# Dense attention on one core: products with values in four column groups once a step, and scores, exponentials and maxima in single PSUM banks

## The chip, the core and the metric

The kernel runs on one core of a Trainium2 chip. The metric is the device time of one execution, in microseconds. The program is one launch that holds a whole stack of four blocks, each a half feed-forward part, an attention and a second half feed-forward part.

## The reference

The input x has 4 sequences of 512 rows of 128 features. Every block adds, in turn, half a feed-forward part, an attention and half a feed-forward part, each of the normalized x. Three of these parts hold a *dense* attention with 16 heads of 8 features, and only these are touched here: both feed-forward parts of block 1 (causal, followed by a mixture of 8 experts of which two count) and the attention of block 3 (without a mask).

The lines are block 1's; block 3 has them without the two that make and apply the mask.

```python
scores = jnp.einsum('bhqd,bhkd->bhqk', q, k) * scale
causal = jnp.tril(jnp.ones((S, S), dtype=bool))
scores = jnp.where(causal[None, None], scores, -jnp.inf)
attn = jax.nn.softmax(scores, axis=-1)
ctx = jnp.einsum('bhqk,bhkd->bqhd', attn, v).reshape(B, S, E)
attn_out = ctx @ out_proj_w.T + out_proj_b
```

All is in 32-bit floats. The other parts (gated and pattern feed-forwards, linear, blocked and local attentions) keep their instructions.

## The kernel before

Features lie on the 128 partitions. A head has 8 features; four heads fill a group of 32 partitions, and there are four such groups g. For each of four j, a copy of the keys is kept in which only head j of every group is non-zero (L712 to L723, "marked keys"), so that a product over the 32 partitions of one group gives the scores of one head. A *unit* u is a sequence b and a j, thus four heads, one in each group; there are 16 units. A unit has four *steps* (one block of 128 keys each, kt), and a step has two *halves*, of groups 0, 1 and of groups 2, 3.

`dense_attention` (L748) is a loop over steps n, from -5 on, and over halves. In each half it does in this order, and TensorE keeps the order in which products are written (`mm_in_order`, L163):

- `scores` (L799): two products of a 32x128 block of marked keys with 32x512 queries, for the groups of this half, into the two banks of one PSUM tile `pk_at`, of which there is one (`k=1`).
- `maxima` (L764): for the step five later (LEAD) and for the *other* half's groups, two products of queries with marked keys into the two banks of one tile `pq_at` (`q=2`), from which VectorE takes row maxima into `nm`: one reduction over both banks without a mask (L780), or two masked ones (L785).
- `weights` (L812): ScalarE takes the exponential of the pair in one instruction (L815) into `PT` in SBUF; in the masked case GpSimd then sets the part above the diagonal to 0 (L818).
- `with_values` (L823): for the step before, two products of 128x32 values with `PT`, whose 32-column results go to the column groups g of one bank `po_at` (`o=1`), and add up over the unit's four steps.
- What has been put off (`later`, L870 on, and the chains of `tick`, L265): transposes of the maxima for the queries of the next unit (`queries`, pm_at, L790), the end of a unit (`end`, pt_at, L838), loading of the next sequence (`prepare`), and the experts, normalizations and gates (L968 on).

The masked case treats only what is not masked: score widths go 512, 384, 256, 128 in a unit's four steps. All PSUM is in use: `MIX = dict(k=1, q=2, o=1, m=1)`, where k and q count double banks; m is one bank for everything else. The products of the experts (`products`, L1020) take one of the two `q` tiles, as two halves, and VectorE adds them up in eight instructions (L1033) before the tile is free. Near the start and the end of masked loops, products that nobody reads (`idle_product`, L169) run in a bank of `o` or `q`. The gated feed-forward of block 3 takes a double bank `pag` (L1799) from a pool of its own.

A helper writes every product, so nearly all products carry line L164, and transposes L161.

Of the kernel before, what the change touches and what calls it, by code (L numbers as in the profile page):

```python
# [24 lines left out]
AF = mybir.ActivationFunctionType  # L25
# [78 lines left out]
def tile_macaron(ctx, tc, x_in, const_in, vec_in, w0_in, ws_in, ws3_in, w2f_in, w3_in, out):  # L104
# [15 lines left out]
            yield  # L120

    def bank(tag, name):
        n = 2 if tag in "kqd" else 1
        return psum["pool"].tile([P, n * 512], F32, tag=tag, name=name, bufs=psum["bufs"][tag])

    x = keep.tile([P, NT, D], F32, name="x")
    w0 = keep.tile([P, WA], F32, tag="wa", name="w0")
# [35 lines left out]
    def mm_in_order(dst, lhsT, rhs, start=True, stop=True):  # L163
        tc.keep_in_program_order(nc.tensor.matmul(dst, lhsT=lhsT, rhs=rhs, start=start, stop=stop))  # L164
# [60 lines left out]
    def by_order(i):  # L225
        if ordered["act"]:
            tc.keep_in_program_order(i)
# [477 lines left out]

    LEAD = 5
    VW = HD + 1
    MIX = dict(k=1, q=2, o=1, m=1)  # L710

    def marked_keys(sb, src, bias):  # L712

# [34 lines left out]
    def dense_attention(sb, prepare, finish, wo, masked, tiles=None):  # L748
# [15 lines left out]
        def maxima(step, half):  # L764

            (b, j), qt = units[step // TB], order[step % TB]
            qT, km = seqs[b]["q"], seqs[b]["k"]
            nk = (qt + 1) * P if masked else S
            pq = bank("q", "pq_at")
            for i in range(2):  # L770
                g = half * 2 + i
                mm_in_order(
                    pq[:, i * 512 : i * 512 + nk],
                    qT[32 * g : 32 * g + 32, ts(qt, P)], km[32 * g : 32 * g + 32, j, :nk],
                )
            nm = nms[j % 2]
            if not masked:
                a = nm[:, qt, 0:1]
                to = bass.AP(a.tensor, a.offset + 64 * half + HD * (j ^ 1), [list(a.ap[0]), [32, 2]])
                nc.vector.tensor_reduce(to, pq.rearrange("p (i n) -> p i n", i=2), AX.X, ALU.max)  # L780
                return
            for i in range(2):
                at = 64 * half + 32 * i + HD * (j ^ 1)
                s = sb.tile([P, S], F32, tag="s", name="s")
                nc.vector.tensor_tensor_reduce(  # L785
                    s[:, :nk], pq[:, i * 512 : i * 512 + nk], causal[:, S - nk :], 1.0, -BIG, ALU.add, ALU.max,
                    nm[:, qt, at : at + 1],
                )

        def queries(u):  # L790
            b, j = units[u]
# [7 lines left out]
        def scores(step, half):  # L799

            u, kt = step // TB, step % TB
            b, j = units[u]
            q0 = kt * P if masked else 0
            pk = bank("k", "pk_at").rearrange("p (i n) -> p i n", i=2)
            for i in range(2):
                g = half * 2 + i
                mm_in_order(
                    pk[:, i, q0:], seqs[b]["k"][32 * g : 32 * g + 32, j, ts(kt, P)], qxs[u][32 * g : 32 * g + 32, q0:]
                )
            return pk  # L810

        def weights(step, half, pk):  # L812
            q0 = step % TB * P if masked else 0
            PT = sb.tile([P, 2, S], F32, tag="PT", name="PT", bufs=4)
            by_order(nc.scalar.activation(PT[:, :, q0:], pk[:, :, q0:], AF.Exp, scale=SC8))  # L815
            if masked:
                d = PT[:, :, q0 : q0 + P]
                nc.gpsimd.affine_select(  # L818
                    d, d, pattern=[[0, 2], [1, P]], base=0, channel_multiplier=-1, compare_op=ALU.is_ge, fill=0.0
                )  # L820
            PTs[step, half] = PT

        def with_values(step, half):  # L823
            u, kt = step // TB, step % TB
            b, j = units[u]
            q0 = kt * P if masked else 0
            if kt == 0 and half == 0:
                pos[u] = bank("o", "po_at")
            PT = PTs.pop((step, half))
            for i in range(2):  # L830
                g = half * 2 + i
                at = (4 * g + j) * VW
                mm_in_order(
                    pos[u][32 * g : 32 * g + 32, q0:], seqs[b]["vh"][:, kt, at : at + 32], PT[:, i, q0:],
                    kt == 0, kt == TB - 1,
                )

# [47 lines left out]

        for n in range(-LEAD, n_steps + 5):
            for half in range(2):
                pk = scores(n, half) if 0 <= n < n_steps else None
                if n + LEAD < n_steps:
                    maxima(n + LEAD, 1 - half)  # L890
                if masked and n < 0:
                    idle_product("o", S // 2)
                elif masked and routed and n_steps - LEAD <= n < n_steps:
                    idle_product("q", S // 2)
                if pk is not None:
                    weights(n, half, pk)
                if 1 <= n <= n_steps:
                    with_values(n - 1, half)
                    if half and n % TB == 0:
                        u = n // TB - 1  # L900
                        oTs[u] = sb.tile([P, S], F32, tag="oT", name="oT")
                        by_order(nc.scalar.copy(oTs[u], pos.pop(u)))
                fs = later.pop((n, half), ())
                tick(bool(fs))
                for f in fs:
                    f()
# [61 lines left out]
    def l1_experts(sb, b):  # L968
# [49 lines left out]
            nc.vector.tensor_add(yb, yb, pb.rearrange("p (t d) -> p t d", d=D))  # L1018

        def products(t):  # L1020
            if "e" in psum["bufs"]:
                pe = [bank("e", "pe1") for _ in range(2)]
            else:
                p = bank("q" if "q" in psum["bufs"] else "d", "pe1")
                pe = [p[:, 0:512], p[:, 512:1024]]
            for half in range(2):
                mm_in_order(pe[half], yT[:, b, ts(t, P)], ew[:, ts(half, 512)])
            st["pe", t] = pe
# [544 lines left out]
    def l3_ffn(w3, tag, first, rb):  # L1573
        with pool(tag) as sb, banks(tag + "ps", d=3, m=2):
# [5 lines left out]
            def W(l, name):  # L1580
                return W3(w3, f"{name}{l}")
# [4 lines left out]
            def act(*args, **kw):  # L1586
                tc.keep_in_program_order(nc.scalar.activation(*args, **kw))  # L1587
# [2 lines left out]
                tc.keep_in_program_order(nc.scalar.copy(dst, src))  # L1590

            def pair(name):
                return bank("d" if "d" in psum["bufs"] else "q", name)

            def light(u):

# [81 lines left out]
            def weights(step):  # L1678

                u, t = step // TB, step % TB  # L1680
                qT, kT = s_state[step].pop("qT"), u_state[u]["kT"]
                ps = pair("ps3")
                for fc in range(4):
                    for w in range(2):
                        for r in range(2):
                            at = r * 512 + fc * P
                            k0 = t * P + w * 64
                            mm_in_order(
                                ps[64 * w : 64 * w + 64, at : at + P],
                                qT[64 * r : 64 * r + 64, fc, ts(w, 64)], kT[64 * r : 64 * r + 64, fc, k0 : k0 + P],  # L1690
                            )
# [101 lines left out]
            def hidden(u, c, at=whole):  # L1793
                l, b = units[u]
                a, n = HCH[c]
                h2, w1, m = u_state[u]["h2"][:, at], W(l, "w1"), at.stop - at.start
                if c == 0 and at.start == 0:
                    u_state[u]["hh"] = rb.tile([P, 3, S], F32, tag="hh", name="hh")
                p = pair("pag")  # L1799
                mm_in_order(p[:n, 0:m], w1[:, HID + a : HID + a + n], h2)  # L1800
                mm_in_order(p[:n, 512 : 512 + m], w1[:, a : a + n], h2)
                ge = tmp("ge")
                act(ge[:n, :m], p[:n, 0:m], AF.Gelu, bias=W(l, "b1g")[:n, c : c + 1])
                nc.vector.scalar_tensor_tensor(
                    u_state[u]["hh"][:n, c, at], p[:n, 512 : 512 + m], W(l, "b1a")[:n, c : c + 1], ge[:n, :m], ALU.add, ALU.mult
                )

            def close_unit(u, at=whole):
# [252 lines left out]
```

## Time and profile before

| what | before |
|---|---|
| median of 3 runs | 2833.52 us (2828.96 to 2839.0) |
| the profiled execution, its own time | 2852.98 us |
| its span | 2851.2 us, mean granted clock 0.886 |
| PE, DVE, ACT, POOL busy | 2254.2, 1806.5, 1245.4, 907.3 us |
| first and last pk of the masked attentions | 415.4 to 720.0 us, 901.1 to 1204.6 us |
| first and last pk of the unmasked attention | 2087.4 to 2423.1 us |
| exponentials (L815), all three | 384 instructions, 311.1 us |
| masked maxima (L785), unmasked maxima (L780) | 512 in 248.5 us, 128 in 156.4 us |

PE is TensorE's matrix products, PEld its loads of weights, DVE VectorE, ACT ScalarE, POOL GpSimd. A row of the timeline has the start, the duration, the engine, the line, the operation, what it writes and reads, the shapes, how many instructions are merged into the row, and in brackets how long the engine was idle before it and who ended that. A product in 32-bit floats appears as two MATMUL records. A row of groups has the count, then busy time and mean duration in ns, and after the second bar the idle time before them with those who ended it. PE's durations contain the way through the array, so that rows overlap; the distance between starts tells how fast it takes work.

### The profile page before, as it was taken

How to read it: one execution, taken by the hardware profiler on the slowest of the kernel's cores; microseconds unless marked ns; L12 is line 12 of the kernel's file. 1: busy time of each engine (PE TensorE's matmuls, PEld its weight loads, DVE VectorE, ACT ScalarE, POOL GpSimd, SP SyncE). 2: the span in 40 equal slices, each digit the busy share in tenths (PEclk: the TensorE clock that was granted, in tenths of full speed). 3: DMA queues.
4: the chain of work that ended last, by engine and by line, in shares of the span. 5: the costliest groups of instructions: out<-in, count | busy, mean ns of one | idle time of the engine just before them, and what ended most of it. 6: DMA issues, size and time to landing. Idle time of an engine off the chain costs nothing. (4 is left out here: it accounts for less than half of the span.)

```text
span 2851.2 us, 47230 instructions
## 1 busy us (share of the span) xinstructions
PE 2254.2 (79%) x17676; PEld 1181.4 (41%) x17676; DVE 1806.5 (63%) x4885; ACT 1245.4 (44%) x2683; POOL 907.3 (32%) x1678
## 2 busy tenths in 40 slices
PE   4377468988678898958666768898799999688988
PEld 2155123333334333338456645555322222455555
DVE  4745576675676676463664497777566564777774
ACT  3054314433333433314332256776334444567674
POOL 1023012232122222203322377676200000677661
PEclk8588769998789998968886889999899999999998
DMA  3052010000000000008104511000000000110000
GB/s 137 9 162 68 0 60 1 1 1 1 1 1 1 1 1 5 4 16 290 38 13 174 169 25 24 20 22 16 1 0 1 1 1 1 27 23 20 22 22 12
DMA packets 33917, 99.15 MB, mean 35 GB/s; under 512 B 6200, under 2 KB 12344, under 8 KB 33176
## 3 DMA queue, kind: packets, MB, share of 16 engines
q1 hardware_dynamic: 30760, 88.03, 9.5%
q0 software_dynamic: 2496, 5.12, 0.8%
q8 instruction: 139, 2.28, 0.3%
q10 hardware_dynamic: 432, 2.98, 0.3%
q14 instruction: 90, 0.74, 0.1%
HBM read 66.88 MB, written 14.55 MB: 29 GB/s over the span
## 5 line engine op out<-in xcount | busy, mean ns | idle before, releaser
L815 ACT ACTIVATE PT<-pk_at 128x1024 f32<-128x1024 f32 (+3 forms) x384 | 311.1, 810 | 546.7 <-PE pq_at L164 466.7
L164 PE MATMUL pk_at<-qx,km 32*128 32x512 f32 (+3 forms) x1536 | 366.2, 553 | 58.5 <-ACT PT L815 53.3
L164 PE MATMUL po_at<-PT,vh 128*32 128x512 f32 (+3 forms) x1536 | 329.0, 510 | 4.4 <-POOL PT L818 4.2
L785 DVE CUSTOM_DVE_ANT_0 s<-pq_at,cst 128x384 f32<-128x384 f32 (+3 forms) x512 | 248.5, 485 | 93.9 <-PE pq_at L164 82.4
L1587 ACT ACTIVATE s<-s,nm,rn 128x128 f32<-128x128 f32 x512 | 245.5, 482 | 2.5 <-POOL ir L191 1.9
L818 POOL TENSOR_SCALAR_AFFINE_SELECT PT<-PT 128x256 f32<-128x256 f32 x256 | 106.9, 419 | 417.6 <-ACT PT L815 417.4
L164 PEld LDWEIGHTS pk_at<-qx,km 32*128 32x128 f32 x1536 | 118.8, 188 | 260.7 <-ACT PT L815 198.3
L164 PE MATMUL pq_at<-km,qT 32*128 32x128 f32 (+3 forms) x1024 | 218.4, 503 | 7.6 <-DVE y L1033 3.9
L780 DVE TENSOR_REDUCE nm<-pq_at 128x2 f32<-128x1024 f32 x128 | 156.4, 1225 | 92.1 <-PE pq_at L164 91.9
L1648 POOL TENSOR_TENSOR t<-t,t 128x1024 f32<-128x1024 f32 x64 | 151.7, 2371 | 127.7 <-DVE t L1644 127.4
L161 PE MATMUL pt_y<-ident,y 128*128 128x128 f32 x224 | 52.0, 359 | 136.4 <-DVE y L218 91.5
L164 PE MATMUL p_qk<-w,hT 128*128 128x512 f32 x256 | 137.9, 665 | 16.2 <-DVE hT L1605 9.0
L164 PE MATMUL pq_at<-km,t 32*128 32x512 f32 x512 | 147.5, 653 | 2.0 <-DVE nm L780 2.0
L164 PEld LDWEIGHTS po_at<-PT,vh 128*32 128x32 f32 x1536 | 55.7, 109 | 221.3 <-issue 146.2
L161 PE MATMUL pt<-ident,s 128*128 128x128 f32 x640 | 93.8, 294 | 61.7 <-POOL s L1711 37.4
L1711 POOL TENSOR_TENSOR s<-s,sm 128x1024 f32<-128x1024 f32 x64 | 121.6, 1900 | 49.8 <-DVE sm L1710 41.8
L247 ACT COPY yT<-pt_y 128x512 f32<-128x512 f32 x56 | 32.8, 586 | 235.2 <-PE pt_y L161 235.1
L1587 ACT ACTIVATE sq<-p_qk 128x1024 f32<-128x1024 f32 x64 | 65.7, 1026 | 120.9 <-PE p_qk L164 67.3
L161 PEld LDWEIGHTS pt<-ident,s 128*128 128x128 f32 x640 | 78.8, 151 | 94.1 <-POOL s L1711 48.6
L1641 DVE TENSOR_TENSOR t<-p_qk,w 128x1024 f32<-128x1024 f32 x64 | 78.2, 1222 | 52.9 <-ACT sq L1587 52.6
L1329 DVE SCALAR_TENSOR_TENSOR hT<-pa,w,sg 128x128 f32<-128x128 f32 x184 | 51.8, 345 | 87.4 <-ACT sg L1328 65.5
L161 PEld LDWEIGHTS pt_y<-ident,y 128*128 128x128 f32 x224 | 33.3, 169 | 168.1 <-issue 96.1
(435 smaller groups left out, 5202.5 us busy)
## 6 DMA issues: line engine op xcount, KB each, us to landing
w<-in_w2f_dram SPq DMA_DIRECT2D x46, 836.0 KB, 7.7
vb<-v SPq DMA_DIRECT2D x112, 128.0 KB, 2.2
skew<-qe SPq DMA_DIRECT2D x16, 512.0 KB, 3.0
rel<-skew SPq DMA_DIRECT2D x64, 128.0 KB, 3.7
w<-in_w_dram SPq DMA_DIRECT2D x1, 4147.0 KB, 12.5
w<-in_w_dram SPq DMA_DIRECT2D x1, 3200.0 KB
od<-o SPq DMA_DIRECT2D x46, 64.0 KB, 5.5
yd<-y SPq DMA_DIRECT2D x8, 256.0 KB
```

What stands on the lines that cost most here:

```text
L161: return nc.tensor.transpose(dst, src, ident[: src.shape[0], : src.shape[0]])
L164: tc.keep_in_program_order(nc.tensor.matmul(dst, lhsT=lhsT, rhs=rhs, start=start, stop=stop))
L247: by_order(nc.scalar.copy(yT[:, b, :], pt))
L780: nc.vector.tensor_reduce(to, pq.rearrange("p (i n) -> p i n", i=2), AX.X, ALU.max)
L785: nc.vector.tensor_tensor_reduce(s[:, :nk], pq[:, i * 512 : i * 512 + nk], causal[:, S - nk :], 1.0, -BIG, ALU.add, ALU.max, nm[:, qt, at ...
L815: by_order(nc.scalar.activation(PT[:, :, q0:], pk[:, :, q0:], AF.Exp, scale=SC8))
L818: nc.gpsimd.affine_select(d, d, pattern=[[0, 2], [1, P]], base=0, channel_multiplier=-1, compare_op=ALU.is_ge, fill=0.0)
L1329: nc.vector.scalar_tensor_tensor(hT[s][:, c, :], pa[:, ts(c, P)], b1[:, c : c + 1], sg, ALU.add, ALU.mult)
L1587: tc.keep_in_program_order(nc.scalar.activation(*args, **kw))
L1641: nc.vector.tensor_mul(by_head(t1), by_head(p3), over(tab[:, 0]))
L1648: nc.gpsimd.tensor_add(t1, t1, t2)
L1711: nc.gpsimd.tensor_mul(s, s, bcast(sm, P))
```

## The change

- `k` and `q` become single banks, three of each (`MIX = dict(k=3, q=3, o=1, m=1)`): the same eight banks.
- Every group's scores have a bank of their own, and so have its maxima. Exponentials and unmasked reductions are one instruction per bank (twice as many, half as wide).
- `with_values` is called once a step, after half 1's scores and maxima, with all four groups.
- `two_banks` hands out two banks: halves of a double bank where the pool has `d`, else two single ones. The experts' products and `pag` use it. For `pag` and for the experts outside of the dense attentions that is what they had.

```diff
-        n = 2 if tag in "kqd" else 1
+        n = 2 if tag == "d" else 1
...
+    def two_banks(name):
+
+        if "d" in psum["bufs"]:
+            p = bank("d", name)
+            return p[:, 0:512], p[:, 512:1024]
+        return [bank("e" if "e" in psum["bufs"] else "q", name) for _ in range(2)]
...
-    MIX = dict(k=1, q=2, o=1, m=1)
+    MIX = dict(k=3, q=3, o=1, m=1)
...
-            pq = bank("q", "pq_at")
-            for i in range(2):
+            nm = nms[j % 2]
+            pqs = [bank("q", "pq_at") for _ in range(2)]
+            for i, pq in enumerate(pqs):
                 g = half * 2 + i
...
+                mm_in_order(pq[:, :nk], qT[32 * g : 32 * g + 32, ts(qt, P)], km[32 * g : 32 * g + 32, j, :nk])
...
-                nc.vector.tensor_reduce(to, pq.rearrange("p (i n) -> p i n", i=2), AX.X, ALU.max)
...
+                    nc.vector.tensor_reduce(to, pq, AX.X, ALU.max)
...
-            pk = bank("k", "pk_at").rearrange("p (i n) -> p i n", i=2)
-            for i in range(2):
+            pks = [bank("k", "pk_at") for _ in range(2)]
+            for i, pk in enumerate(pks):
...
-            by_order(nc.scalar.activation(PT[:, :, q0:], pk[:, :, q0:], AF.Exp, scale=SC8))
+            for i, pk in enumerate(pks):
+                by_order(nc.scalar.activation(PT[:, i, q0:], pk[:, q0:], AF.Exp, scale=SC8))
...
-        def with_values(step, half):
+        def with_values(step):
...
-            PT = PTs.pop((step, half))
-            for i in range(2):
-                g = half * 2 + i
+            PT = [PTs.pop((step, half)) for half in range(2)]
+            for g in range(4):
                 at = (4 * g + j) * VW
                 mm_in_order(
-                    pos[u][32 * g : 32 * g + 32, q0:], seqs[b]["vh"][:, kt, at : at + 32], PT[:, i, q0:],
+                    pos[u][32 * g : 32 * g + 32, q0:], seqs[b]["vh"][:, kt, at : at + 32], PT[g // 2][:, g % 2, q0:],
                     kt == 0, kt == TB - 1,
                 )
...
-                if 1 <= n <= n_steps:
-                    with_values(n - 1, half)
-                    if half and n % TB == 0:
+                if half and 1 <= n <= n_steps:
+                    with_values(n - 1)
+                    if n % TB == 0:
...
-            if "e" in psum["bufs"]:
-                pe = [bank("e", "pe1") for _ in range(2)]
-            else:
-                p = bank("q" if "q" in psum["bufs"] else "d", "pe1")
-                pe = [p[:, 0:512], p[:, 512:1024]]
+            pe = two_banks("pe1")
...
-                p = pair("pag")
-                mm_in_order(p[:n, 0:m], w1[:, HID + a : HID + a + n], h2)
-                mm_in_order(p[:n, 512 : 512 + m], w1[:, a : a + n], h2)
+                pg, pa = two_banks("pag")
+                mm_in_order(pg[:n, :m], w1[:, HID + a : HID + a + n], h2)
+                mm_in_order(pa[:n, :m], w1[:, a : a + n], h2)
```

More of the change, by code (lines that the diff above doesn't have):

```diff
@@ L768, in maxima @@
             nk = (qt + 1) * P if masked else S
-            pq = bank("q", "pq_at")
-            for i in range(2):
+            nm = nms[j % 2]
+            pqs = [bank("q", "pq_at") for _ in range(2)]
+            for i, pq in enumerate(pqs):
                 g = half * 2 + i
[L772 to L781, printed above, removed]
-            for i in range(2):
-                at = 64 * half + 32 * i + HD * (j ^ 1)
[L784 to L788, printed above, removed]
+                mm_in_order(pq[:, :nk], qT[32 * g : 32 * g + 32, ts(qt, P)], km[32 * g : 32 * g + 32, j, :nk])
+            for i, pq in enumerate(pqs):
+                at = 64 * half + 32 * i + HD * (j ^ 1)
+                to = nm[:, qt, at : at + 1]
+                if masked:
+                    s = sb.tile([P, S], F32, tag="s", name="s")
+                    nc.vector.tensor_tensor_reduce(s[:, :nk], pq[:, :nk], causal[:, S - nk :], 1.0, -BIG, ALU.add, ALU.max, to)
+                else:
+                    nc.vector.tensor_reduce(to, pq, AX.X, ALU.max)
         def queries(u):
@@ L803, in scores, with weights @@
             q0 = kt * P if masked else 0
-            pk = bank("k", "pk_at").rearrange("p (i n) -> p i n", i=2)
-            for i in range(2):
+            pks = [bank("k", "pk_at") for _ in range(2)]
+            for i, pk in enumerate(pks):
                 g = half * 2 + i
                 mm_in_order(
-                    pk[:, i, q0:], seqs[b]["k"][32 * g : 32 * g + 32, j, ts(kt, P)], qxs[u][32 * g : 32 * g + 32, q0:]
+                    pk[:, q0:], seqs[b]["k"][32 * g : 32 * g + 32, j, ts(kt, P)], qxs[u][32 * g : 32 * g + 32, q0:]
                 )
-            return pk
-        def weights(step, half, pk):
+            return pks
+        def weights(step, half, pks):
             q0 = step % TB * P if masked else 0
             PT = sb.tile([P, 2, S], F32, tag="PT", name="PT", bufs=4)
-            by_order(nc.scalar.activation(PT[:, :, q0:], pk[:, :, q0:], AF.Exp, scale=SC8))
+            for i, pk in enumerate(pks):
+                by_order(nc.scalar.activation(PT[:, i, q0:], pk[:, q0:], AF.Exp, scale=SC8))
             if masked:
@@ L826, in with_values @@
             q0 = kt * P if masked else 0
-            if kt == 0 and half == 0:
+            if kt == 0:
                 pos[u] = bank("o", "po_at")
-            PT = PTs.pop((step, half))
-            for i in range(2):
-                g = half * 2 + i
+            PT = [PTs.pop((step, half)) for half in range(2)]
+            for g in range(4):
                 at = (4 * g + j) * VW
                 mm_in_order(
-                    pos[u][32 * g : 32 * g + 32, q0:], seqs[b]["vh"][:, kt, at : at + 32], PT[:, i, q0:],
+                    pos[u][32 * g : 32 * g + 32, q0:], seqs[b]["vh"][:, kt, at : at + 32], PT[g // 2][:, g % 2, q0:],
                     kt == 0, kt == TB - 1,
@@ L1592, in pair @@
             def pair(name):
-                return bank("d" if "d" in psum["bufs"] else "q", name)
+                return bank("d", name)
             def light(u):
@@ L1798, in hidden @@
                     u_state[u]["hh"] = rb.tile([P, 3, S], F32, tag="hh", name="hh")
-                p = pair("pag")
-                mm_in_order(p[:n, 0:m], w1[:, HID + a : HID + a + n], h2)
-                mm_in_order(p[:n, 512 : 512 + m], w1[:, a : a + n], h2)
+                pg, pa = two_banks("pag")
+                mm_in_order(pg[:n, :m], w1[:, HID + a : HID + a + n], h2)
+                mm_in_order(pa[:n, :m], w1[:, a : a + n], h2)
                 ge = tmp("ge")
-                act(ge[:n, :m], p[:n, 0:m], AF.Gelu, bias=W(l, "b1g")[:n, c : c + 1])
+                act(ge[:n, :m], pg[:n, :m], AF.Gelu, bias=W(l, "b1g")[:n, c : c + 1])
                 nc.vector.scalar_tensor_tensor(
-                    u_state[u]["hh"][:n, c, at], p[:n, 512 : 512 + m], W(l, "b1a")[:n, c : c + 1], ge[:n, :m], ALU.add, ALU.mult
+                    u_state[u]["hh"][:n, c, at], pa[:n, :m], W(l, "b1a")[:n, c : c + 1], ge[:n, :m], ALU.add, ALU.mult
                 )
```

## The prediction

> **What bounds the kernel now.** I read the page first, then the table of windows for the three dense attentions, then the timeline of one half step, then the groups by shape for the prices.
>
> The page says that PE is busy for 79% of 2851.2 us and no other engine for more than 63%; the profiled execution took 2852.98 us, 0.7% over the median 2833.52 of the runs. The change touches three windows only:
>
> ```profile
> 415.00:720.00 305.00, 271.57 (x1812) 103.54 (x1811) 194.61 (x765) 120.08 (x191) 86.48 (x205) 0.94 0.00 1
> 901.00:1205.00 304.00, 273.51 (x1830) 105.32 (x1829) 190.66 (x744) 118.83 (x188) 82.81 (x202) 0.95 0.01 3
> 2087.00:2424.00 337.00, 312.05 (x1710) 84.46 (x1712) 191.56 (x255) 146.12 (x156) 8.89 (x7) 0.99 0.00 1
> ```
>
> The columns are length, then PE, weight loads, DVE, ACT, POOL busy, then the granted clock. PE is busy for 89 to 93% in each: two masked attentions (305 and 304 us) and the unmasked one (337). How a half step of the unmasked one looks (first column the start, second the duration; the weight loads are left out):
>
> ```profile
> 2152.52 0.70 PE L164 MATMUL pk_at<-qx,km 32*128 32x512 f32 x2 [0.19 <-ACT PT L815]
> ...
> 2152.53 0.70 PE L164 MATMUL pq_at<-km,t 32*128 32x512 f32 x2
> ...
> 2153.05 0.59 PE L164 MATMUL pk_at<-qx,km 32*128 32x512 f32 x2
> 2153.06 0.59 PE L164 MATMUL pq_at<-km,t 32*128 32x512 f32 x2
> ...
> 2153.59 1.05 PE L164 MATMUL po_at<-PT,vh 128*32 128x512 f32 x4
> 2153.75 1.23 DVE L780 TENSOR_REDUCE nm<-pq_at 128x2 f32<-128x1024 f32 x1 [1.09 <-PE pq_at L164]
> 2153.75 1.02 ACT L815 ACTIVATE PT<-pk_at 128x1024 f32<-128x1024 f32 x1 [1.29 <-PE pq_at L164]
> ...
> 2154.83 0.70 PE L164 MATMUL pk_at<-qx,km 32*128 32x512 f32 x2 [0.19 <-ACT PT L815]
> ```
>
> Each fp32 product is two passes. Two pk and two pq lie in four row groups and run together: passes begin 0.53 us apart, 1.07 us for all four products. The two po follow in two column groups, also together. Their individual starts are 0.453 us apart per pass, so 0.91 us. PE has then issued 1.98 us of work, and the next pk, which needs the only pk tile, waits until the exponentials of the whole pair have ended. The loop is 1.07 + 0.16 (drain and signal, 2153.59 to 2153.75) + 1.02 + 0.06 = 2.31 us; PE lacks work for 0.33 of it.
>
> From the starts of pk in the timeline, undisturbed steps take 4.62, 4.95, 4.62, 4.95 us in the unmasked attention (19.14 a unit of four; 0.33 twice for the transposes pm and pt) and 4.62, 4.31, 2.92, 2.61 in a masked one (14.46). Sixteen units make 306 and 231 us; the remaining 30 and 74 us are other work of PE in between, a halved clock (about 31 us in each masked window, some 15 us lost), and stalls.
>
> **The change, part by part.**
>
> Products with values. Removed: one of two issues of two column groups per step; added: one issue of four. If four groups run together as two do, a 512-wide step saves 0.91 us. The trace has four groups elsewhere, 128 wide:
>
> ```profile
> 873.33 0.86 PE L164 MATMUL po_1a<-PT,vm 128*32 128x128 f32 x24
> ```
>
> 24 passes in 0.86 us, the last one's drain within it; individual rounds of four start 0.109 us apart (serially 24 x 0.109 = 2.6). [...] I take the row: its rounds show no loss, only its width is other. The moved half-0 products go behind half 1's pk and pq on PE; their PT is a step old, so no wait is added, and oT's copy by ACT follows the fourth product as before.
>
> Banks. A pk bank now comes round every third product, so the fourth product of a step waits for the first one's exponential, where a pair used to wait for the pair. Prices:
>
> ```profile
> L815 ACT ACTIVATE PT<-pk_at 128x1024 f32<-128x1024 f32 x32 | 32.8, 1024 | 65.3 <-PE pq_at L164 52.9 <-PE pk_at L164 10.1 <-POOL PT L818 2.3
> L815 ACT ACTIVATE PT<-pk_at 128x512 f32<-128x512 f32 x32 | 19.1, 596 | 47.5 <-PE pq_at L164 38.8 <-PE pk_at L164 7.2 <-POOL ln_r L198 1.4
> ```
>
> Two of 596 for one of 1024: +0.168 us a pair, 256 x 0.168/2 = 21 us more ACT in the unmasked window (146 of 337 busy, so on no path). DVE's one reduce of 1226 ns becomes two, not shown by the trace; bounds are 0.61 (half) and 0.75 us (the dearest 512-wide DVE row there); I take 0.69, as tensor-tensor rows have at 512 and 1.22 at 1024. [...]
>
> Unmasked step after, from its first pk (t = 0). Half 0 issues until 1.07. Its first exponential runs 1.23 to 1.83, its first reduce 1.23 to 1.92. pk of the third group starts at 1.07 in a fresh bank; the fourth waits for the exponential until 1.88; the first pq behind it needs no more, the second pq waits for the reduce until 1.98. Behind these waits are queued the products with values and all other PE work of the slot; exponentials and reduces of half 1 wait for them too. A later row group may join a running one: at 682 us pq start 0.89 us after pk and pk's second pass begins on time. Half 1 ends at 3.05, four po at 3.96, and the change from column to full mode took 0.08 (po to pt_y, 523.97 to 524.96). So 4.04 us. pt adds 0.6; pm falls into the stall of half 1 and is free (0.6 if DVE is late). Unit: 4 x 4.04 + 0.6 = 16.8 against 19.1: 16 x 2.4 = -38 us.
>
> Masked, by the same chain with rows of their widths (exponentials 0.60, 0.49, 0.38, 0.27; reduces 0.69, 0.54, 0.42, 0.29; pk and pq 1.07, 0.85, 0.64, 0.43; po, a step late, 0.27, 0.91, 0.69, 0.48): 3.4, 4.2 with pt, 2.7, 2.1, together 12.4 against 14.5: 16 x 2.1 = -34 us each. Reduces were separate here before, so DVE has nothing more to do.
>
> What is given back. PE is in order, so lateness of DVE stops it. Before, a pq pair waited for the pair two back (in the unmasked loop some 2.1 us of slack); after, a bank for the third back (0.1 us at worst). Expert products (L1024) took one of two pq tiles and now take two of three banks: the fourth pq after them waits for four of eight sums of 0.35 us. Tracing two cases, I get 0.4 to 1.0 us lost a call, some 12 us a masked window. Other DVE bursts (normalization, choice, km): 60 us of DVE extras a masked window, of which I let a third stall, less what deeper pk banks save when ACT is late: 5 us. Unmasked: 27 us of DVE extras, mostly in bursts, some 4 us net. So -34 + 17 = -17 for each masked window, and -38 + 4 = -34 unmasked. (The other way about, masked: 198 for 16 clean units; 47 of other PE work, counted from the order of instructions at 0.96 to 1.07 a 128x512 product and 0.13 a transpose, of which 20 stand in half 0 and 6 of these hide in the stall; 15 of clock; 28 of stalls, of which some 12 are there now too: 288 against 305.) Bounds: nothing lost (-34, -38) to all DVE extras stalling.
>
> The gated FFN's pag, now through two_banks, gets the same two halves of the same tile and its instructions stay: nothing. The idle products take one bank instead of two, at equal length: nothing. No DMA moves.
>
> Sum: 2 x -17 - 34 = -68 us on the span, carried to the median: 2765 us.
>
> **The rivals.**
>
> 1. DVE lateness decides, slower. All 60 us of DVE extras of a masked window stop PE, and PE's pauses drop the clock: masked 198 + 41 (the 47 less the hidden 6) + 15 + 60 = 314, plus 15 us for twice the cold time: +24 each. Unmasked 268 (16 x 16.8) + 15 (other PE work, 22 less what hides) + 27 = 310: -26. Total +22: 2856. It decides from about 50 us of PE stall per masked window. For it: slack falls to 0.1 us. Against: DVE is busy for only 64%, and PE's waits for DVE are a few us now. Chance 14%.
> 2. The stalls of half 1 fill with the other PE work and bursts hide: masked -40 each, unmasked -45: 2708. Chance 14%.
> 3. [...] Chance 9%.
> 4. It does not do what it says: half 1's waits cost what the po saving brings, 2834. Chance 6%.
> The likeliest, 2765 (2740 to 2800), has 57%.
>
> **How the numbers follow.** A measurement here tells about 0.3% (8.5 us) from no change. Faster by more: likeliest, 2 and 3, 80%; within: 6%; slower: 14%. The range leaves out the far half of rivals 1 and 2: 2708 to 2834.
>
> **What would show it.** After, po should come as eight passes within about 1.05 us, once a step; one pk alone at 1.07 us, its fellow with two pq at 1.9; undisturbed unmasked steps of 4.0 us; windows of about 288, 287 and 303 us. Wrong would be: four po passes of 0.6 us or more apart; PE idle before pq on nm, s or y (DVE) of over 50 us a masked window; a clock under 0.9 there.

## The result, and the profile after

The changed kernel takes 2807.05 us (median of 5 runs, 2792.72 to 2815.06); five runs of the kernel before, the three shown among them, give 2838.25. The ratio is 0.9872 with an interval of 0.9852 to 0.9893: faster by 1.3%, some 31 us in medians, where 68 were forecast. The direction was right, the size about half. Two later measurements of the same pair give 46 and 42 us.

The profiled executions lie further apart than the medians, 2852.98 and 2795.84 us: before's is 14.7 us above the median of its five runs, after's is 11.2 below its own. So 57 us between the two profiles stand for about 31. Some 10 of the 57 lie between the second masked attention and the unmasked one, which the change leaves as it was: that stretch took 882.8 us before, 872.4 here, and 883.2 in both later profiles of the changed kernel. Only what repeats is built on below.

The three windows again, with the same columns (length; PE, weight loads, DVE, ACT, POOL busy; granted clock), each from the first to the last pk of an attention, now of the kernel after:

```profile
416.00:704.00 288.00, 268.86 (x1811) 121.91 (x1814) 200.03 (x767) 129.43 (x319) 86.80 (x205) 0.92 0.00 1
881.00:1184.00 303.00, 285.67 (x1825) 129.66 (x1817) 194.53 (x740) 129.35 (x315) 82.99 (x202) 0.86 0.01 3
2056.00:2364.00 308.00, 290.77 (x1701) 103.73 (x1700) 198.07 (x374) 154.49 (x282) 8.90 (x7) 0.97 0.00 1
```

The first masked attention went from 305 to 288 us, as forecast. The second, which does the same work, stayed at 303 (287 forecast). The unmasked one went from 337 to 308 (303 forecast). The column that moves the wrong way is the clock: 0.94, 0.95, 0.99 before, now 0.92, 0.86, 0.97. It fell most where the gain is missing. And PE is *busier* in the second masked window than before (285.67 against 273.51 us), though the change packs its products with values into less time: instructions at half clock last longer and count as busy (below, eight passes of po in 1.70 us instead of 1.07).

One undisturbed step of the unmasked attention, from the timeline of after (start, duration; weight loads and a few rows left out):

```profile
2107.88 0.70 PE L171 MATMUL pk_at<-qx,km 32*128 32x512 f32 x2
2107.90 0.70 PE L171 MATMUL pq_at<-km,t 32*128 32x512 f32 x2
...
2108.86 1.52 PE L171 MATMUL pk_at<-qx,km 32*128 32x512 f32 x3
2109.04 1.57 ACT L817 ACTIVATE PT<-pk_at 128x512 f32<-128x512 f32 x3 [2.22 <-PE pq_at L171]
2109.13 1.29 DVE L789 TENSOR_REDUCE nm<-pq_at 128x1 f32<-128x512 f32 x2 [0.55 <-PE pq_at L171]
2109.70 0.87 PE L171 MATMUL pq_at<-km,t 32*128 32x512 f32 x2
...
2110.92 1.07 PE L171 MATMUL po_at<-PT,vh 128*32 128x512 f32 x8
2111.92 0.70 PE L171 MATMUL pk_at<-qx,km 32*128 32x512 f32 x2
```

The step has the form that was worked out, and its length: 2107.88 to 2111.92 is 4.04 us. The fourth pk waits for the first exponential, and from 2108.86 one pk runs alone, joined at 2109.70 by pq. Eight passes of po in four column groups take 1.07 us; two groups took 1.05 for four passes. Three exponentials in a row are merged into 1.57 us, so consecutive ones overlap; two reductions take 1.29.

So the undisturbed steps are right, and the loss lies elsewhere. I cut each attention into its 63 steps from one step's first pk to the next one's, and took from the records of granted clock how long each step ran at half clock:

| attention | 63 steps, before to after, us | at half clock, us | steps at full clock in both: number, change | the other steps: change |
|---|---|---|---|---|
| first masked | 301.5 to 283.0 | 34 to 43 | 50: -16.7 us | 13: -1.7 us |
| second masked | 301.1 to 301.3 | 31 to 82 | 41: -16.3 us | 22: +16.5 us |
| unmasked | 332.8 to 306.0 | 5 to 16 | 59: -29.4 us | 4: +2.6 us |

Carried over to all 63 steps, the steps at full clock gain 21, 25 and 31 us (16.7 x 63/50 and so on), together 77. What was had is 45 (the sums of the second column). The steps that ran at half clock in one kernel or the other took the 32 us between.

This is how such a stretch begins: a burst in the unmasked attention, from the timeline of after. Normalization (y), key copies (km) and maxima stand in line on DVE:

```profile
2158.11 2.12 DVE L225 TENSOR_SCALAR y<-x,ln_mv,ln_r 128x128 f32<-128x128 f32 x4
...
2160.15 0.99 DVE L729 TENSOR_SCALAR km<-t,cst 128x512 f32<-128x512 f32 x2
...
2161.07 2.58 DVE L789 TENSOR_REDUCE nm<-pq_at 128x1 f32<-128x512 f32 x4
2161.80 0.69 PE L171 MATMUL pq_at<-km,t 32*128 32x512 f32 x1 [1.96 <-DVE nm L789]
...
2164.04 1.70 PE L171 MATMUL po_at<-PT,vh 128*32 128x512 f32 x8
```

PE waits 1.96 us for a maximum that stands behind the burst; from about 2164 the same eight passes of po take 1.70 us instead of 1.07. The table of windows for three stretches of 4 us around it:

```profile
2156.00:2160.00 4.00, 3.39 (x19) 0.76 (x16) 3.97 (x10) 1.81 (x4) 1.26 (x1) 1.00 0.01 2
2160.00:2164.00 4.00, 2.20 (x10) 1.13 (x10) 3.77 (x8) 3.13 (x6) 0.00 (x0) 1.00 0.00 0
2164.00:2168.00 4.00, 3.23 (x14) 1.34 (x14) 1.69 (x4) 0.41 (x1) 0.00 (x0) 0.54 0.00 0
```

DVE is busy all the time (3.97, 3.77 of 4), PE falls to 2.20 of 4, and 0.54 is the clock of the next 4 us. That the pause brings the low clock is the reading of this place, which shows only the order; what the 25 falls of the clock in the two profiles show follows after the experiments.

How much of the pauses is DVE's lateness, by the table of waits (weight loads in front of pq; us in all, times, longest), first masked attention before:

```profile
PEld pq_at L164 <- DVE y L1033: 5.0, 6, 1.4
PEld pq_at L164 <- DVE nm L785: 4.5, 5, 1.9
```

and after:

```profile
PEld pq_at L171 <- DVE nm L787: 17.7, 21, 3.2
```

9.5 us became 17.7; in the second masked attention 7.5 became 15.3, in the unmasked one 3.7 became 12.8. That is 8 to 9 us more in each, far from the 50 of rival 1, and alike in the two masked attentions. It cannot be what parts 288 from 303. Over all weight loads that wait for DVE, not only those before pq, the three went from 27, 26 and 10 us to 32, 29 and 27: 3 to 4 us more in a masked attention, 17 in the unmasked one.

### The profile page after: what moved, and what is told of

The parts are those of the page before. It is cut to its first block, busy times and chain, and to the rows that moved or that the text cites. A ratio compares the mean times of both kernels' runs of the same rounds, so it can differ in the third digit from the quotient of the medians.

```text
span 2793.4 us, 48072 instructions
## 1 busy us (share of the span) xinstructions
PE 2243.8 (80%) x17676; PEld 1246.5 (45%) x17676; DVE 1820.5 (65%) x5013; ACT 1274.0 (46%) x3067; POOL 909.6 (33%) x1678
## 4 chain that ended last, share of the span: by engine, by line
PE 56%; DVE 23%; POOL 8%; ACT 7%; issue 5%; DMA 2%; POOLq 0%; DVEq 0%; SPq 0%; ACTq 0%
PE pk_at L171 12%; PE po_at L171 5%; PE pq_at L171 4%; PE pa L171 3%; PE pag L171 3%; PE po L171 3%; PE pe L171 2%; DVE t L1638 2%; DVE t L1641 2%; PE p_qk L171 2%; PE pg L171 2%; PE pz L171 2%; PE pv L171 2%; PE pt L168 2%; POOL t L1645 2%
## 5 line engine op out<-in xcount | busy, mean ns | idle before, releaser
L817 ACT ACTIVATE PT<-pk_at 128x512 f32<-128x512 f32 (+3 forms) x768 | 337.3, 489 | 453.1 <-PE pq_at L171 376.1
L171 PE MATMUL pk_at<-qx,km 32*128 32x512 f32 (+3 forms) x1536 | 453.6, 563 | 12.2 <-ACT PT L817 10.0
L171 PE MATMUL pq_at<-km,qT 32*128 32x128 f32 (+3 forms) x1024 | 279.9, 525 | 16.7 <-DVE nm L787 13.7
L171 PEld LDWEIGHTS pk_at<-qx,km 32*128 32x128 f32 x1536 | 170.2, 195 | 226.3 <-ACT PT L817 119.2
L789 DVE TENSOR_REDUCE nm<-pq_at 128x1 f32<-128x512 f32 x256 | 165.2, 684 | 64.3 <-PE pq_at L171 63.5
L171 PE MATMUL po_at<-PT,vh 128*32 128x512 f32 (+3 forms) x1536 | 173.6, 526 | 0.0
L171 PE MATMUL pq_at<-km,t 32*128 32x512 f32 x512 | 166.8, 657 | 6.5 <-DVE nm L789 6.5
L171 PEld LDWEIGHTS pq_at<-km,qT 32*128 32x128 f32 x1024 | 109.4, 197 | 53.5 <-DVE nm L787 35.5
```

The lines of the kernel that those rows point to most:

```text
L789: nc.vector.tensor_reduce(to, pq, AX.X, ALU.max)
L817: by_order(nc.scalar.activation(PT[:, i, q0:], pk[:, q0:], AF.Exp, scale=SC8))
```

## The experiments

My theory after the result: the steps come out as worked, and the missing half goes to the clock, which falls since PE, with less to do, more often pauses. (The last clause did not hold as it stands. By the windows of before and after PE's idle time, the length less its busy time, was 33, 30 and 25 us before and is 19, 17 and 17 after.) Rivals: DVE's lateness itself (the experts' sums above all), and that one of the two parts does not bring what it should.

**The products with values alone.** Before's banks, with the four groups once a step:

```diff
-        def with_values(step, half):
+        def with_values(step):
...
-                if 1 <= n <= n_steps:
-                    with_values(n - 1, half)
-                    if half and n % TB == 0:
+                if half and 1 <= n <= n_steps:
+                    with_values(n - 1)
+                    if n % TB == 0:
```

> The kernel before, with only the products with values changed: once a step, after half 1, in all four column groups; the double banks stay. Theory (the loop from a pk tile through the exponential of the pair and back sets the step, 2.31 us a half): clean unmasked steps stay at 4.62 us, PE only idles longer in half 0, and the time stays within 0.4% of before. Rival (the column groups are the gain): 0.9 us a step less in the unmasked attention, some 30 us in all.

It takes 2846.83 us against 2841.3 (20 and 23 runs): 1.0016 (1.0007 to 1.0026). The timeline of half 1, then the next half 0, without values in between:

```profile
2116.41 0.70 PE L164 MATMUL pk_at<-qx,km 32*128 32x512 f32 x2 [0.17 <-ACT PT L815]
...
2117.64 1.02 ACT L815 ACTIVATE PT<-pk_at 128x1024 f32<-128x1024 f32 x1 [1.29 <-PE pq_at L164]
2118.72 0.70 PE L164 MATMUL pk_at<-qx,km 32*128 32x512 f32 x2 [1.17 <-ACT PT L815]
```

A half is still 2.31 us (2116.41 to 2118.72), since the exponential of the pair closes the loop. The 0.91 us of PE that the column groups save became idle time: PE now waits 1.17 us here instead of 0.19. And the clock is lower, by the table of windows (first masked, unmasked):

```profile
417.00:722.00 305.00, 249.55 (x1806) 102.00 (x1798) 195.16 (x760) 120.19 (x191) 86.66 (x205) 0.88 0.00 1
...
2074.00:2418.00 344.00, 268.95 (x1698) 80.46 (x1700) 191.68 (x252) 146.15 (x155) 8.91 (x7) 0.93 0.00 1
```

PE's busy time fell from 271.57 to 249.55 and from 312.05 to 268.95 us, the clock from 0.94 to 0.88 and from 0.99 to 0.93. Time at half clock in the three attentions' steps went from 34, 31, 5 to 70, 58, 43 us. Steps at full clock in both kernels gained 9.0, 10.8 and 7.9 us (41, 44, 55 steps), the others lost 8.1, 9.8 and 15.1. So what the steps at full clock gained, 28 us, the others lost again, 33 us.

**The banks alone.** After, with the values twice a step again, two groups each:

```diff
-        def with_values(step):
+        def with_values(step, half):
...
-                if half and 1 <= n <= n_steps:
-                    with_values(n - 1)
-                    if n % TB == 0:
+                if 1 <= n <= n_steps:
+                    with_values(n - 1, half)
+                    if half and n % TB == 0:
```

> The changed kernel, with products with values once a half in two column groups again. Theory: PE's 1.98 us a half plus some 0.1 for the change of mode set the pace, since the wait for the first exponential (1.88 us) is over when the two po are issued: clean unmasked steps of 4.15 to 4.2 us against 4.04 of the whole change, so the banks alone bring most of the gain, 20 to 30 us. Rival (column groups are the gain): as before, 2838 us.

2819.44 us against 2841.3: 0.9915 (0.9886 to 0.9944). Its windows:

```profile
418.00:713.00 295.00, 281.57 (x1812) 111.59 (x1810) 199.60 (x767) 128.12 (x318) 86.29 (x205) 0.96 0.00 1
893.00:1188.00 295.00, 285.35 (x1825) 114.99 (x1824) 195.00 (x745) 126.89 (x315) 82.75 (x202) 0.96 0.01 3
2055.00:2388.00 333.00, 320.35 (x1704) 88.10 (x1701) 198.89 (x373) 154.13 (x282) 8.87 (x7) 0.96 0.00 1
```

Undisturbed unmasked steps take 4.11 and 4.69 us, with no wait for the exponential left in the middle of a half. PE is busy 95 to 97% of every window, and both masked attentions are alike, with a clock of 0.96. The same finer buffers, with the same nearness of DVE, but without the saving on PE, hold the clock: 24, 24 and 26 us at half clock, about as much in all as before. Here 0.85% (22 us, as expected most of the gain), in the whole change 1.3 to 1.7% in three measurements, and in the values alone nothing: in the whole time the parts do not add up. In the steps at full clock they come closer: 28 us for the values alone, 22 for the banks alone (4.5, 3.4 and 14.6 in 52, 54 and 59 steps), 62 for both. What hides the values' share when they stand alone is the clock.

**The values between the halves.** After, with the four groups put after half 0:

```diff
-                if half and 1 <= n <= n_steps:
+                if not half and 1 <= n <= n_steps:
```

> The changed kernel, with the four products with values after half 0's scores and maxima instead of after half 1's, to fill PE's wait there. If that wait were a loss that any work fills: unmasked steps of 3.1 to 3.3 us, 45 us less than the changed kernel. Theory (three banks for four products: the second product of the next step waits for this step's third exponential, 1.89 us after half 1 begins): the wait only moves to the next half 0, steps of 3.95 us, the time within 10 us of the changed kernel's 2807.

2793.82 us: 0.9832 (0.9799 to 0.9865). Undisturbed unmasked steps come in a pattern of 3.36, 4.62, 4.04 and 4.72 us, 16.74 us for four, as much as in the changed kernel: the wait only moved, as expected. The windows are 289.8, 284.3 and 320.5. The second masked attention is now the good one (34 us at half clock in its steps, the first 58), and the unmasked one loses (47). A shift of one instruction group moves the spells of half clock from one attention to another, with little change in the total: where they fall is not a property of the second masked attention.

**Work for PE in the pauses.** After, with a product that nobody reads in front of half 1's pk, in a bank that this pk overwrites, so that it fills the wait for the exponential. First in all three attentions:

```diff
+            if half:
+                w = (S - q0) // 2
+                mm_in_order(pks[0][:, q0 : q0 + w], onesm, cst[:, :w])
```

> The changed kernel with one more product a step that nobody reads (full array, half the width of the scores), ahead of half 1's first score product and into its bank, where PE else runs one row group alone or waits. Theory (what is missing of the forecast is the clock, 113 us at half clock in the masked windows against 60 before): less than 70 us of half clock in the masked windows and 15 to 25 us less than the changed kernel. Rival (lateness of VectorE itself is what is missing): the clock is up, the time within 5 us of the changed kernel, clean steps at 4.04 us in both cases.

2782.94 us: 0.9796 (0.9770 to 0.9823), with windows of 284.7, 289.6 and 315.5 us and 58 us at half clock in the masked steps, where the changed kernel has 125. Then only where there is a mask (`if half and masked`):

> The changed kernel with the unread product of the first filled kernel in the two masked attentions only. Theory (the fill pays through the clock, and the unmasked attention was warm without it: there the fill only delays): the unmasked attention is back at about 308 us, the masked ones at 285 to 290, 7 us less than with the fill everywhere: 2776 us. Rival (the fill pays through something other than the clock): no less than with the fill everywhere, 2783 us or more.

2779.67 us against 2837.32: 0.9792 (0.9768 to 0.9817). The unmasked attention is back at 308 us, but the ratio is that of the filling everywhere; the 7 us expected are not shown. On another chip, side by side with the plain change:

> The changed kernel once more, beside the fill on one chip. Theory (clock): mean granted clock about 0.87 against 0.888 before, ratio 0.982 to 0.988.

> The changed kernel with the fill in the masked attentions, on the same chip as the changed kernel. Theory (what is missing is the clock): mean clock 0.88 or more, undisturbed warm steps no shorter, and 0.4 to 0.9% (11 to 25 us) less time than the changed kernel in runs on the same chip. Rival (the gain of the fill was a difference between chips): the same ratio as the changed kernel within 0.2%.

2792.01 us (2786.72 to 2796.49) with the extra products and 2805.36 (2800.49 to 2813.19) without: 13.4 us or 0.48% faster with *more* work for PE, and the runs of the two do not overlap. The windows with the extra products:

```profile
416.00:701.00 285.00, 269.33 (x1936) 127.04 (x1928) 199.55 (x765) 127.70 (x318) 86.25 (x205) 0.96 0.00 1
877.00:1168.00 291.00, 276.88 (x1947) 130.94 (x1944) 194.93 (x742) 126.67 (x315) 82.55 (x202) 0.94 0.01 3
2052.00:2359.00 307.00, 289.72 (x1699) 104.20 (x1696) 197.69 (x373) 154.61 (x282) 8.91 (x7) 0.97 0.00 1
```

In the second window there are 122 more matmul records than in after's (x1947 against x1825), and it is 12 us shorter, at 0.94 instead of 0.86. Steps at full clock in both got 3.1 and 2.2 us dearer in the two masked attentions, the others 4.9 and 14.5 us cheaper; the unmasked attention, which has no extra products, was 6.7 us shorter in this profile than in its companion's, about as much as it differs between profiles of one kernel (308 and 314.6). An edit that adds work and takes none away makes the stages shorter just in the steps that ran at half clock; these went from 125 to 59 us of it in the masked attentions. A mere shift of instructions does a part of that: with the values between the halves, and no added work, it was 92. The filling gets back 13 us, not all of the missing 37.

**The same filling in the kernel before**, as a control:

```diff
+            if half and masked and 0 <= step - LEAD:
+                mm_in_order(pq[:, : nk // 2], onesm, cst[:, : nk // 2])
```

> The kernel before with an unread product of half the width ahead of the maxima's products of groups 2 and 3, in the masked attentions only, as a control of the fill. Theory (the clock is what the change lost there): the kernel before is at half clock for only 65 us in its masked windows, so the fill gains less than 5 us, or costs up to 10 since it adds PE work. Rival (the fill helps any version): 15 us less than before or better.

2926.09 us: 1.0318 (1.0291 to 1.0345). It is no control for the filling, since it costs more than either forecast allowed, and the timeline shows why:

```profile
545.22 0.91 PE L164 MATMUL pk_at<-qx,km 32*128 32x384 f32 x4
546.06 0.59 PE L164 MATMUL pq_at<-cst,onesm 128*128 128x192 f32 x2
546.58 0.92 PE L164 MATMUL pq_at<-km,qT 32*128 32x384 f32 x4
```

A product over all 128 rows between pk and pq parts the two pairs, which otherwise run side by side in four row groups: pq begins 1.36 us after pk instead of at once. Its clock did rise (27 and 20 us at half clock in the masked windows), and the time did not follow. The filling paid where it stood in a wait, and cost where it parted products that ran together.

**Without the experts' sums.** Both kernels with one of the eight sums (the other seven are left out, so the experts' output is not the reference's):

```diff
-            for e in range(n):
+            for e in range(1):
```

> The changed kernel, leaving out seven of the eight sums over experts of every 128 rows (the second and later ones of L1030). Theory (the experts' sums hold two of three q banks and make VectorE late, some 12 us a masked window): against the kernel before with the same sums left out, 50 to 60 us less, where the full kernels differ by 31 to 36. Rival (lateness is from other bursts, or the clock): the difference stays at 31 to 36 us.

> The kernel before, leaving out seven of the eight sums over experts of every 128 rows: the other half of the comparison. By either theory shorter than before by what VectorE's sums cost alone outside the attentions (32 rows blocks of 2.4 us, less in the windows where PE is the bound): 20 to 60 us; masked windows 290 to 300 us.

After becomes 2751.01 us, before 2797.99: a ratio of 0.983, while the whole kernels have 0.9872, 0.9826 and 0.9841 in three measurements. If the sums took the gain, the change would have to bring clearly more without them. It brings 47 us, below the 50 to 60 of the theory and above the 31 to 36 of the rival; the whole kernels differ by 31, 46 and 42. At most it brings a little more. The masked windows are 285.1 and 277.5 (after), 298.3 and 293.3 (before): 13 and 16 us apart, where the whole kernels are 17 and 0 apart. The second one is again a matter of the clock (38 us at half clock in its steps instead of 82). So my 12 us for the sums are not shown.

**Shorter bursts on DVE.** With the filling, and the normalizations' scaling (`y`, four instructions) on ACT:

```diff
-            scaled(y, x, b, st[0], pinned)
+            if ordered["act"]:
+                scaled_by_act(y, x, b, st[0])
+            else:
+                scaled(y, x, b, st[0], pinned)
...
```

> The changed kernel with the fill in the masked attentions, and inside the three dense attentions the last step of every normalization (four scalings of 0.35 us) done by ScalarE instead of VectorE. Theory (bursts of VectorE work stop PE through the q banks): the longest steps (10.8 and 10.4 us unmasked, 11.3 masked) get 1 to 2 us shorter, six to nine bursts in all, 8 to 15 us less than the fill alone: some 2768 us. Rival (bursts are hidden, or ScalarE's lateness takes their place through the k banks): 2775 to 2790 us.

2794.59 us, 0.9812 (0.9788 to 0.9837), where the filling alone had 0.9792 and 0.9799: no gain. The longest steps are 10.4 us unmasked and 10.0 masked, where the theory started from 10.8 and 11.3 and asked for 1 to 2 us less. To shorten one link of a burst was not enough.

**Both moves together**, the values between the halves and the filling, in masked attentions:

> The changed kernel with, in the masked attentions only, the products with values between the halves and the fill ahead of half 0's first score product. If the clock is what the version with values between the halves lost in its first masked window (58 us at half clock): masked windows of 275 to 283 us and 2765 us in all. If the wait that moves to half 0 is what counts: as the fill alone, 2775 to 2785 us.

2802.81 us, 0.9827 (0.9800 to 0.9855), with windows of 289.4, 288.5 and 314.6: no more than either. The plain change, run beside these two:

> The changed kernel itself, on the same chip as the next two and the kernel before. By the fit of time against clock (2 us for 0.001 in both kernels): a mean granted clock some 0.02 under that of the kernel before, and a ratio of 0.985 to 0.99.

2805.34 us, 0.9826 (0.9793 to 0.9858), with windows of 287.8, 303.1 and 314.6 us. So the first profile's 288 and 303 repeat in the masked attentions, down to the time at half clock (43 and 82 us in all three profiles of this kernel), while its 308 in the unmasked one was a good case. The third profile's row for that one:

```profile
2068.00:2382.00 314.00, 296.74 (x1699) 105.62 (x1696) 198.30 (x373) 154.77 (x282) 8.90 (x7) 0.95 0.00 1
```

The same instructions were granted 0.97 in the first profile and 0.95 here, 16 us at half clock against 33. The 57 steps at full clock in both differ by 0.0 us in sum; the other 6 take 6.2 us more. That is the clearest evidence for the clock: one kernel, one attention, and only the clock and the time of the steps under it differ. It also gives a price, 6.2 us for 16.4, or 0.38 us for each us at half clock.

## Why the prediction was half right

- **Undisturbed steps** (4.04 unmasked; 3.4, 4.2, 2.7, 2.1 masked): the unmasked ones are right, 4.04, with pt 4.62 where 4.64 was worked out; pm is indeed free, and a unit takes 16.74 against 16.8. In the masked ones 3.38, 4.07, 2.71 and 2.10 all occur, but not in one unit: after a first step of 3.38 the second takes 4.39 to 4.60, so that the best units take 12.6 and 12.8 against 12.4. There pq waits for maxima, which follow each other on DVE 0.84 us apart (from 462.71 to 463.55 us, for one: 0.69 of the maximum itself, the reading of the accumulator until 463.41, and 0.14 more), where the chain had 0.69.
- **Four column groups** at the price of two, taken from the row of 128-wide products (24 passes in 0.86 us): right. No run shows rival 3's term, a dearer issue at 512 columns (0.23 us a step, 2799 in all): eight passes in four groups took 1.06 to 1.07 us, where four passes in two groups took 1.05. Rival 3 falls.
- **Smaller reads of PSUM**: right that they lie on no path, too dear in size. Two exponentials of 512 take 1.09 us, not 2 x 0.596, against 1.02 for one of 1024; two reductions take 1.29, not 1.38, against 1.23. That is 0.07 + 0.06 us a pair, 17 us for 128 pairs, where the prediction's prices, 0.17 and 2 x 0.69 - 1.23 = 0.15 us a pair, make 41. In the unmasked window ACT's busy time rose by 8.4 us, DVE's by 6.5.
- **What is given back to DVE**, 17 us a masked window: the waits before pq grew by 8 there and all waits of weight loads for DVE by 3 to 4, so 17 was too much. In the unmasked one, where 4 net were assumed, they grew by 9 and 17, so 4 was too little. The share of 12 for the sums is not shown.
- **The step that failed** is the term of the clock. The masked cross-sum carried "15 of clock" over from the kernel before, so the change itself got nothing for it, without a reason, and the unmasked window had no term at all. Time at half clock in the steps of the three attentions went from 70 to 141 us (158 in the two later profiles). At the 0.38 us found above, the 71 us more cost some 27 us, and the 88 us more some 33 (estimates); the windows fell short of the forecast 68 by 24 and by 30. The table of steps gives 32. One of the prediction's own signs of being wrong, a clock under 0.9 in a masked window, came true (0.86). Without the clock the steps at full clock give 77, beyond the 68; but the steps left out hold more of the bursts, so 77 is an upper figure.
- **A slip in the cross-sum**: 198, 47, 15 and 28 make its 288, but 6 of the 47 were said to be hidden, and rival 1 takes them off. With 41 it is 282, so the two ways of reckoning did not agree as well as it seemed.
- **By window** it was -17, -17, -34. It became -17, 0 and -27 in the first profile, and about -21 (314.6 against 335.7, first to last pk) for the last in later ones. The first is right only in its sum, by luck: a larger gain (21 by the steps at full clock), less 3 in the others.
- **Rival 1** (slower, 2856) had the falling clock, from PE's pauses (the ten falls of before do come behind 1.09 to 3.38 us of busy PE in 4, below), and let the time at half clock double, which it did overall (70 to 141). Its other half was wrong: it asked for 60 us of stalls a masked window, and 15 to 18 were found before pq.

The medians point the same way. The mean granted clock of a whole run is 0.889 before (median of 23 runs) and 0.869 after. Among runs of one and the same kernel, 0.001 of clock goes with 1.8 to 2.2 us of time (before, values alone, after). So 0.020 are some 40 us, and 31 + 40 is about the 68 that were forecast. This is a correlation over runs, not a proof; the two profiles of one kernel above are the nearest to an experiment that changes the clock alone.

**Why the clock fell**, though PE idles less in the windows, no run shows; this is what was measured. In the three attentions the granted clock fell from full to half 10 times before and 15 times after. In the 4 us ahead of a fall PE was busy for 2.5 us in the mean before (1.09 to 3.38) and for 2.8 after (2.04 to 3.27, and once 4.00), where the whole windows have 89 to 94%, thus 3.6 to 3.8 us in 4. So 24 of these 25 falls came behind a stretch in which PE had paused more than it does on average; the profiles show the order, not a rule for how long a pause it takes.

Between kernels, the time at half clock went with the way in which the values are multiplied. Twice a step, in two column groups, the three attentions had 70 us at half clock with the old banks (before) and 74 with the new ones (the banks alone); once a step, in four groups, 171 (the values alone) and 141 (after). Falls came 10 and 7 times there, and 23 and 14 or 15 times here. Packing four groups into one issue halved the time for which po ran: 97, 96 and 132 us of the three windows before, 50, 52 and 68 after. The extra products, which add work, went with 10 falls and with 59 instead of 125 us at half clock in the masked attentions. PE's busy share of a whole window does not sort the cases: after's second masked window is busy for 94% at 0.86, the one with extra products for 95% at 0.94. That the clock falls because po runs for less time is the author's reading of these numbers. It came afterwards; no run was made to test it, or to tell it from the pauses.

Not shown: how the pauses for DVE and the clock share the loss exactly, since in the burst shown the low clock begins where DVE was late.

## What to carry to other kernels

A chain of starts and waits, written out for one undisturbed step, came out to 0.02 us in the unmasked attention and to 0.4 in the masked one; do it before a sum over whole stages, and follow it through a whole unit. Two edits to one loop need not add: the values alone brought nothing, the banks alone 0.85%, both 1.3 to 1.7%. When an edit packs PE's products into less time and other waits remain, put a lower clock into the sum, as an estimate (here 0.94 became 0.88 with the values alone, and 0.95 became 0.86 in the whole change's second masked window), and look at the granted clock in the rows of the stage; a product that nobody reads, placed in a wait, bought back 0.5% here.

## What the hardware showed beyond that

The granted clock is either full or half in every record of the profiles of before and after (124 and 138 records), nothing between; the fractions in the rows are means over time (0.95 is a tenth of the time at half clock). The kernel is 13 us faster with some 250 extra matmul records in its masked attentions. Consecutive instructions of one kind overlapped by about 0.1 us on ACT and DVE (two exponentials of 596 ns in 1.09 us, two reductions of 684 ns in 1.29), which took most of the price off splitting a read of PSUM: 0.07 us a pair of exponentials instead of 0.17.
